# Batch 0's softmax denominators: summed two score tiles later, kept in the room of x's sums, the last group inside the projection

## The chip, the core and the metric

The kernel runs on one core of a Trainium2 chip. The metric is device microseconds of that core; lower is better. Everything is float32.

## What is computed

Two layers on x of shape (4, 1024, 32, 32): four batches, 1024 channels, 1024 tokens each. Only the first layer matters here.

```python
qkv = (x @ w_qkv.T + b_qkv).reshape(B, N, 3, nh, hd)      # 16 heads of 64
q, k = rmsnorm(rope(q)) * q_norm_w, rmsnorm(rope(k)) * k_norm_w
scores = einsum('bqhd,bkhd->bhqk', q, k) * hd ** -0.5
attn = softmax(scores, axis=-1)                           # exp / sum of exp
ctx = einsum('bhqk,bkhd->bqhd', attn, v)
out = rmsnorm(ctx @ w_proj.T, norm_out_w) + residual
```

The second layer (1x1, 3x3 and 1x1 convolutions with batch norms) follows and is not touched.

## The kernel before

Per batch the kernel projects q, k and v (two levels of a Strassen-like scheme, 49 products a matrix from batch 1 on), runs attention, and projects the result (y). Batch b's stages follow each other on PE.

**Attention** (`attention`, called once for each half c of the queries) loops over eight pairs of heads, hp = 0 to 7, so batch 0 has sixteen steps of this kind. In a step PE makes eight score tiles `sc` (keys 128t on, both heads, 512 queries; L781), ACT turns each into exponentials `p` (L788), and VectorE (DVE) adds the eight tiles into a sum `den` (L799 once, L801 six times). Then PE multiplies the exponentials by v into `cx` (L810), ACT copies it out, and GpSimd (POOL) adds the two halves by a DMA (L820).

The exponentials are not divided. Instead the sums are inverted beside the work, and the context is scaled later. In batch 0 this goes by **groups of two steps**, eight groups. After the second step of a group a function is put into the list `late`. The next step takes it out at its second score tile (t == 1): PE sums `den` over the partitions into the PSUM tile `dn` (`sums_of_four`, eight records at L863), ACT copies it to `rec` (L910), and `to_few` sends it to memory (L898, `densf<-rec`) and reads it back spread over 128 partitions (L902, `few<-densf`). Both DMAs are issued by SyncE's queue (SP). At the end of that step DVE inverts `few` (L914). SP writes it back (L915) and reads it into two broadcast tiles `inv` (L932). At the end of the step after that, DVE and POOL scale the context (`mean_of_v`, L764 and L765).

The last group of a batch goes another way (`last_inverses`): `dn` directly behind the last `cx`, copy on ACT (L923), reciprocal on DVE (L924), and DMAs from POOL's queue (L925, L932). Its scaling stands in the projection, at `after(3, means)`.

**Beside the attention of batch 0** the kernel prepares weights for later stages. A part is four 256 KB pieces: SP loads them into a ring of eight buffers (L406, L383), DVE makes four sums (L409 to L412, L392 to L395), POOL writes the four results to memory (L414, L397). `load_parts`, at t == 3, keeps two parts loaded ahead. So a load waits until POOL's DMA has read the buffer's previous content.

**What sets the order.** PE, POOL, DVE and ACT run their instructions in the order in which the program states them. SP is not among these: the planner chooses the order of SP's DMAs when the program is built. That order is then fixed, and SP works through it one by one: a DMA that waits holds up those behind it.

**Rooms.** `den` is a tile of the pool `acc` (tag "tot", two buffers). x's sums T0, T1 and T2 (pool `tp`) are used by the projections of q, k and v, and are free during the attention. In batches 1 to 3 the first half's `den` tiles already stand in T0 and T2 (`fold`). PSUM has three tiles of two banks for `sc`, which `dn` also takes, and one for `cx`; in the projection there are four banks `o1` and four banks `o2`.

**The projection behind the attention** (`project2` for y) starts with two products p1 and p2 on old data. Product `S2` (k == 2) reads sums of the context (`to`, L281 to L284). Half of these need the last steps' scaled context. `after(n, step)` puts a step into a list of due times, and `product_done` runs those that are due after each product. SP loads the products' weights `w_y` through the same ring of eight buffers, and at the same time the next batch's x (L215), whose room holds the exponentials until the last sum and the last `cx` are done.

Of the kernel before, what the change touches and what calls it, by code (L numbers as in the profile page):

```python
# [11 lines left out]
F32 = mybir.dt.float32  # L12
# [6 lines left out]
P = 128  # L19
# [5 lines left out]
CH = 512  # L25
# [36 lines left out]
NH = NT // 2  # L62
# [23 lines left out]
def program(ctx, tc, x, wblk, w2, w3, vecs, cos, sin, out, bad):  # L86
# [71 lines left out]
    with tc.tile_pool(name=f"st{u}", bufs=2) as st, ExitStack() as s:  # L158

        tp = s.enter_context(tc.tile_pool(name=f"tp{u}", bufs=1))  # L160
# [42 lines left out]
        def bank(kind, name):  # L203
            pool, shape = psum[kind]
            return pool.tile(shape, F32, tag=kind, name=name)
# [48 lines left out]
        def after(n, step):  # L254
            later.append((pace["at"] + n, step))
# [508 lines left out]
            nc.vector.tensor_tensor(cx, cx, w, ALU.mult)  # L764
            engine.tensor_scalar(cx, cx, col("bv", hp), None, ALU.add)  # L765

        def attention(b, c, q_all, k_all, v, probs_, late, ready, extra, slow, steps_in_all, load_parts, fold, then):


            at = half[c]  # L770
            sums_, contexts = [], []
            for hp in range(NHP):
                n = f"{b}_{c}_{hp}"
                rows = shifts(q_all, k_all, n, hp, c) if bad is None else None
                probs = []
                for t in range(N // P):
                    p = probs_[:, t]
                    sc = bank("sc", f"sc_{n}_{t}")
                    for keys in (low, high):
                        for j, d in enumerate((low, high)):  # L780
                            nc.tensor.matmul(  # L781
                                sc[keys, j], k_all[d, hp, t * P + keys.start : t * P + keys.stop], q_all[d, hp, at],
                                start=True, stop=bad is not None,
                            )
                    if bad is None:
                        for j in range(2):
                            nc.tensor.matmul(sc[:, j], ones[0:1, :], rows[j], start=False, stop=True)
                    nc.scalar.activation(p, sc, AF.Exp)  # L788
                    if t == 1:
                        if late:  # L790
                            late.pop(0)()
                        if fold and hp % 2 == 0:
                            d_ = fold[hp // 4][:, hp % 4 // 2 * 2 : hp % 4 // 2 * 2 + 2, :]
                        else:
                            d_ = acc.tile([P, 2, CH], F32, tag="tot", name=f"den_{n}")
                    if t == 3:
                        load_parts()
                    if t == 1:
                        nc.vector.tensor_tensor(d_, probs[0], p, ALU.add)  # L799
                    elif t > 1:  # L800
                        nc.vector.tensor_tensor(d_, d_, p, ALU.add)  # L801
                    probs.append(p)
                if (c, hp) == (NCH - 1, NHP - 1):
                    then()
                o = bank("cx", f"cx_{n}")
                for t in range(N // P):
                    for j in range(2):
                        h0 = (2 * hp + j) * HD
                        for i, keys in enumerate((low, high)):
                            nc.tensor.matmul(  # L810
                                o[j * HD : (j + 1) * HD, i], v[keys, t, h0 : h0 + HD], probs[t][keys, j],
                                start=(t == 0), stop=(t == N // P - 1),
                            )

                cx = q_all[:, hp, at]
                nc.scalar.copy(cx, o[:, 0])  # L816
                if b == 0 and (c, hp) != (NCH - 1, NHP - 1):
                    other = temp(f"cx_{n}")
                    nc.scalar.copy(other, o[:, 1])
                    nc.gpsimd.dma_start(cx, other, accum_op=ALU.add)  # L820
                else:
                    contexts.append((cx, o[:, 1]))
                sums_.append(d_)
                if hp % 2 == 1:
                    for r in ready:
                        mean_of_v(q_all, *r)
                    ready.clear()
                if fold:
                    halve(hp, d_, fold[hp // 4][:, hp % 4 // 2 * 2 : hp % 4 // 2 * 2 + 2, :])
                    if hp % 4 == 3:  # L830
                        eights.append((hp + 2, lambda n=n, hp=hp: sum_of_eight(b, n, hp, fold[hp // 4], ready)))
                if half_done and half_done[0][0] <= c * NHP + hp:
                    half_done.pop(0)[1]()
                if slow:
                    slow.pop(0)()

                if waiting:
                    next_waiting()
                slots = NCH * NHP - 1
                if extra and steps_in_all == 0 and hp > 0:  # L840
                    extra.pop(0)()
                for _ in range(len(extra) - -(-steps_in_all * max(slots - 1 - c * NHP - hp, 0) // slots) if steps_in_all else 0):
                    extra.pop(0)()
                if contexts:
                    nc.vector.tensor_tensor(contexts[0][0], *contexts.pop(0), ALU.add)
                if eights and eights[0][0] <= c * NHP + hp:
                    eights.pop(0)[1]()
                if hp % 2 == 0 or fold:
                    continue
                if (c, hp) == (NCH - 1, NHP - 1):  # L850
                    last_inverses(b, c, hp, n, sums_of_four(n, sums_), ready)
                else:
                    late.append(lambda n=n, hp=hp, ds=sums_: inverses(b, c, hp, n, sums_of_four(n, ds), ready))
                sums_ = []

        def sums_of_four(n, sums_):
            if n == f"0_{NCH - 1}_{NHP - 1}":
                bank("sc", f"skip_{n}")
            dn = bank("sc", f"dn_{n}")[:, 0]
            for i, d_ in enumerate(sums_):  # L860
                for j in range(2):
                    q = slice((2 * i + j) * QH, (2 * i + j + 1) * QH)
                    nc.tensor.matmul(dn[q, :], ones[:, :QH], d_[:, j], start=True, stop=True)  # L863
            return dn
# [55 lines left out]
        def last_inverses(b, c, hp, n, dn, ready):  # L920
            k = 2 * ((b * NCH + c) * NHP + hp - 1)
            r = temp(f"rec_{n}")
            nc.scalar.copy(r, dn)  # L923
            nc.vector.reciprocal(r, r)  # L924
            nc.gpsimd.dma_start(dens[k : k + 4, :], r[::QH, :])  # L925
            spread(c, hp, n, ready, [dens[k + j : k + j + 3 : 2, :] for j in range(2)], nc.gpsimd)
# [263 lines left out]
        for b in range(B):  # L1190
            units = units_of(room)
            q_all = kv.tile([P, NT, N], F32, tag="q", name=f"q_{b}")
# [16 lines left out]
            k_all = kp.tile([P, NT, N], F32, tag="k", name=f"k_{b}")  # L1209
# [10 lines left out]
            v = room  # L1220
# [15 lines left out]
            def load_parts():  # L1236

                while todo and len(made) < 2:
                    made.append(todo.pop(0)(pieces, nc.sync))

            extra = [lambda: made.pop(0)()] * len(todo)
            load_parts()
            late, ready, steps_in_all = [], [], len(extra)
# [7 lines left out]
            slow = [lambda: None] * 3 + [lambda f=f: add_residual(f) for f in range(NT)] if b > 0 else []  # L1251
            probs_ = xp.tile([P, N // P, 2, CH], F32, tag="x", name=f"p_{b}")
            fold = [None, None]
            if b > 0:

                fold[0] = [tp.tile([P, NH, CH], F32, tag=t, name=f"den_{b}_{t}") for t in ("T0", "T2")]
            tc_, two = [], []

            def then(b=b, q_all=q_all, tc_=tc_, two=two):
                yt[b] = kp.tile([P, NT, N], F32, tag="k", name=f"y_{b}")  # L1260
                two += [2, *in_place(q_all, tc_, yt[b], False), False]
                for part in range(2):
                    inner_sums(two[1], two[2], 0, part)

            for c in range(NCH):
                if (b, c) == (B - 1, NCH - 1):
                    extra = filters()
                attention(
                    b, c, q_all, k_all, v, probs_, late, ready, extra, slow, steps_in_all, load_parts, fold[c], then
                )  # L1270
            psum_for("proj")
            room = v_room(f"to_{b}")
# [166 lines left out]
        for f in range(NPT):  # L1439
            for c in range(NCH):  # L1440
                then = (first_channels, other_channels)[f] if c == NCH - 1 else None
# [139 lines left out]
        for f in range(NT):  # L1581
# [8 lines left out]
            for i, k in order:  # L1590
                b, c = divmod(i, NCH)
# [14 lines left out]
            sc, sh = norms[f] = norm_of(stats, col("g3", f), col("be3", f), f"3_{f}")  # L1606
# [81 lines left out]
```

## Time and profile before

| what | us |
|---|---|
| three runs | 2668.44, 2664.51, 2668.72 (median 2668.44) |
| the profiled execution | 2665.42, of which its span 2663.6 |
| attention of batch 0, first score tile to last `cx` | 288.6 to 518.2 |
| y projection of batch 0 behind it | 521.7 to 609.1 |
| 285 to 525: busy PE / DVE / ACT / POOL | 238.6 / 220.8 / 141.7 / 90.1 |
| mean share of the DMA engines there | 0.79 |

A line of the timeline gives the start, the time until the end of the group's last instruction, the engine, the source line, the operation, what it writes and reads, the count, and in brackets the idle time ahead of it with what ended it. For SP the idle time is not given: it is read from the starts. A line of the waits gives who waited for whom, the total in us, how often, and the longest. A busy PE is not a PE at its peak: a matmul's end is modelled, so a pause under half a microsecond is not seen as idle time, but in the starts.

### The profile page before, as it was taken

How to read it: one execution, taken by the hardware profiler on the slowest of the kernel's cores; microseconds unless marked ns; L12 is line 12 of the kernel's file. 1: busy time of each engine (PE TensorE's matmuls, PEld its weight loads, DVE VectorE, ACT ScalarE, POOL GpSimd, SP SyncE). 2: the span in 40 equal slices, each digit the busy share in tenths (PEclk: the TensorE clock that was granted, in tenths of full speed). 3: DMA queues.
4: the chain of work that ended last, by engine and by line, in shares of the span. 5: the costliest groups of instructions: out<-in, count | busy, mean ns of one | idle time of the engine just before them, and what ended most of it. 6: DMA issues, size and time to landing. Idle time of an engine off the chain costs nothing.

```text
span 2663.6 us, 40534 instructions
## 1 busy us (share of the span) xinstructions
PE 2628.3 (99%) x15434; PEld 1626.0 (61%) x15434; DVE 2142.2 (80%) x2595; ACT 1120.1 (42%) x1568; POOL 473.4 (18%) x592
## 2 busy tenths in 40 slices
PE   9999999999999999999999999999999999999997
PEld 4448533488888333588886333888884335846843
DVE  5577899988787977788888767887988778877987
ACT  2222465523342655333343655233425654312266
POOL 2542244301001221100111222000111221020000
PEclk9999999999999999999999999999999999999999
DMA  7887788867677452457776541765774443583165
GB/s 271 292 259 214 209 253 240 271 184 242 174 184 215 82 105 48 152 153 221 190 187 162 97 83 28 210 200 180 194 212 90 84 105 132 155 278 100 64 235 208
DMA packets 252793, 463.65 MB, mean 174 GB/s; under 512 B 32176, under 2 KB 124896, under 8 KB 252592
## 3 DMA queue, kind: packets, MB, share of 16 engines
q1 hardware_dynamic: 204736, 304.58, 36.9%
q0 software_dynamic: 47856, 156.40, 23.5%
q8 instruction: 125, 2.05, 0.3%
q14 instruction: 76, 0.62, 0.1%
HBM read 329.53 MB, written 97.01 MB: 160 GB/s over the span
## 4 chain that ended last, share of the span: by engine, by line
PE 66%; DVE 1%; DMA 1%; ACT 0%; issue 0%; ACTq 0%
PE sc L781 13%; PE cx L810 12%; PE p_y L485 9%; PE p_v L480 8%; PE p_k L485 6%; PE p_q L485 6%; PE c L1592 4%; PE c2x L1453 2%; PE c L1015 2%; PE c2y L1453 2%; PE c L974 1%; PE c1s L1015 1%; DMA w_y<-wdf 1%; PE dn L863 0%; DVE V L1388 0%; PE c1a L1015 0%
## 5 line engine op out<-in xcount | busy, mean ns | idle before, releaser
L788 ACT ACTIVATE p<-sc 128x1024 f32<-128x1024 f32 x512 | 478.1, 1049 | 17.8 <-PE sc L781 17.2
L781 PE MATMUL sc<-q,k 64*64 64x512 f32 x4096 | 456.2, 591 | 0.0
L801 DVE TENSOR_TENSOR den<-den,p 128x1024 f32<-128x1024 f32 x312 | 385.6, 1236 | 37.9 <-ACT p L788 5.1
L810 PE MATMUL cx<-p,to 64*64 64x512 f32 x3072 | 338.2, 589 | 0.0
L781 PEld LDWEIGHTS sc<-q,k 64*64 64x64 f32 x4096 | 149.7, 132 | 293.6 <-ACT p L788 149.5
L810 PEld LDWEIGHTS cx<-p,to 64*64 64x64 f32 x3072 | 117.5, 133 | 212.1 <-issue 211.0
L485 PE MATMUL p_y<-q,w_y 128*128 128x256 f32 x928 | 209.8, 379 | 0.7 <-issue 0.7
L480 PE MATMUL p_v<-w_v,x 128*128 128x256 f32 x928 | 209.9, 379 | 0.3 <-DVE x L451 0.3
L485 PEld LDWEIGHTS p_y<-q,w_y 128*128 128x128 f32 x928 | 176.0, 190 | 27.9 <-issue 4.1
L480 PEld LDWEIGHTS p_v<-w_v,x 128*128 128x128 f32 x928 | 176.1, 190 | 25.4 <-DVE x L451 1.2
L816 ACT COPY q<-cx 128x512 f32<-128x512 f32 x64 | 37.5, 585 | 348.1 <-PE cx L810 348.1
L765 POOL TENSOR_SCALAR q<-q,vec 128x512 f32<-128x512 f32 x56 | 110.4, 1985 | 290.5 <-DVE q L764 290.4
L485 PE MATMUL p_q<-to,w_q 128*128 128x256 f32 x672 | 152.2, 379 | 0.0
L485 PE MATMUL p_k<-to,w_k 128*128 128x256 f32 x672 | 152.2, 379 | 0.0
L485 PEld LDWEIGHTS p_k<-to,w_k 128*128 128x128 f32 x672 | 127.4, 190 | 18.4 <-issue 1.2
L485 PEld LDWEIGHTS p_q<-to,w_q 128*128 128x128 f32 x672 | 127.4, 190 | 18.4 <-issue 1.2
L810 PE MATMUL cx<-p,rq 64*64 64x512 f32 x1024 | 112.7, 589 | 0.0
L1592 PE MATMUL c<-h,w 128*128 128x512 f32 x256 | 110.3, 592 | 0.5 <-ACT h L1495 0.5
L485 PE MATMUL p_y<-to,w_y 128*128 128x256 f32 x384 | 90.8, 381 | 9.4 <-issue 5.4
L799 DVE TENSOR_TENSOR den<-p 128x1024 f32<-128x1024 f32 x52 | 63.5, 1222 | 42.5 <-ACT p L788 42.5
L801 DVE TENSOR_TENSOR den_T<-den_T,p 128x1024 f32<-128x1024 f32 x72 | 88.2, 1225 | 7.9 <-DVE den_T L801 0.5
L480 PE MATMUL p_v<-w_v,t 128*128 128x256 f32 x384 | 90.2, 379 | 0.1
(497 smaller groups left out, 4304.8 us busy)
## 6 DMA issues: line engine op xcount, KB each, us to landing
w_v<-wd2f SPq DMA_DIRECT2D x112, 256.0 KB, 3.1
w_y<-wd2f SPq DMA_DIRECT2D x112, 256.0 KB, 2.6
w_q<-wd2f SPq DMA_DIRECT2D x84, 256.0 KB, 2.7
w_k<-wd2f SPq DMA_DIRECT2D x84, 256.0 KB, 2.8
wd2f<-w_pre POOLq DMA_DIRECT2D x68, 256.0 KB, 4.5
x<-in_x_dram SPq DMA_DIRECT2D x64, 256.0 KB, 4.9
q<-qs POOLq DMA_DIRECT2D x64, 256.0 KB, 5.4
k<-ks POOLq DMA_DIRECT2D x64, 256.0 KB, 4.6
```

What stands on the lines that cost most here:

```text
L480: nc.tensor.matmul(o[:, q].rearrange("p (g f) -> p g f", g=2), r[:, i, q * P : (q + 1) * P], wt[:, :, i, :], skip_group_check=True, **at,)
L485: nc.tensor.matmul(o[:, q], wt[:, q, i, :], r[:, i, :], skip_group_check=True, **at)
L765: engine.tensor_scalar(cx, cx, col("bv", hp), None, ALU.add)
L781: nc.tensor.matmul(sc[keys, j], k_all[d, hp, t * P + keys.start : t * P + keys.stop], q_all[d, hp, at], start=True, stop=bad is not None,)
L788: nc.scalar.activation(p, sc, AF.Exp)
L799: nc.vector.tensor_tensor(d_, probs[0], p, ALU.add)
L801: nc.vector.tensor_tensor(d_, d_, p, ALU.add)
L810: nc.tensor.matmul(o[j * HD : (j + 1) * HD, i], v[keys, t, h0 : h0 + HD], probs[t][keys, j], start=(t == 0), stop=(t == N // P - 1),)
L816: nc.scalar.copy(cx, o[:, 0])
L1015: nc.tensor.matmul(o, wt[:, i, :], rows(i), start=first and i == 0, stop=last and i == NH - 1, skip_group_check=True,)
L1453: nc.tensor.matmul(o[:, r * TR * TC : (r + 1) * TR * TC], uw[2 * h + r, j][:, i * PL + f * P : i * PL + (f + 1) * P], vt[b, i][:, 2 * h + ...
L1592: nc.tensor.matmul(os[i], w3t[k][f // NH][:, f % NH, :], h2[b, k][:, half[c]], start=(k == 0), stop=(k == NPT - 1),)
```

## The change

It touches batch 0's attention alone. (1) The function in `late` is taken out at t == 3 in place of t == 1, ahead of `load_parts`. (2) The sums `den` of batch 0 stand in T0 and T2, two steps in each, in place of the two buffers of `acc`; four steps pass until a place is used again. (3) The last group's `dn`, copy, reciprocal and DMAs are put in the list of due times (`after(0.5, ...)`), so that they come behind the projection's first product; `dn` takes a bank of `o2`.

```diff
-        def attention(..., fold, then):
+        def attention(..., fold, then, own):
...
                     nc.scalar.activation(p, sc, AF.Exp)
+                    if t == (3 if b == 0 else 1) and late:
+                        late.pop(0)()
                     if t == 1:
-                        if late:
-                            late.pop(0)()
-                        if fold and hp % 2 == 0:
+                        if b == 0:
+                            d_ = own[hp % 4 // 2][:, hp % 2 * 2 : hp % 2 * 2 + 2, :]
+                        elif fold and hp % 2 == 0:
                             d_ = fold[hp // 4][:, hp % 4 // 2 * 2 : hp % 4 // 2 * 2 + 2, :]
...
                 if (c, hp) == (NCH - 1, NHP - 1):
-                    last_inverses(b, c, hp, n, sums_of_four(n, sums_), ready)
+
+                    def last(ds=sums_):
+                        last_inverses(b, c, hp, n, sums_of_four(n, ds), ready)
+
+                    if b == 0:
+                        after(0.5, last)
+                    else:
+                        last()
...
         def sums_of_four(n, sums_):
             if n == f"0_{NCH - 1}_{NHP - 1}":
-                bank("sc", f"skip_{n}")
-            dn = bank("sc", f"dn_{n}")[:, 0]
+                dn = bank("o2", f"dn_{n}")
+            else:
+                dn = bank("sc", f"dn_{n}")[:, 0]
...
+            own = None
+            if b == 0:
+                own = [tp.tile([P, NH, CH], F32, tag=t, name=f"den_{b}_{t}") for t in ("T0", "T2")]
```

More of the change, by code (lines that the diff above doesn't have):

```diff
@@ L765, in mean_of_v, with attention @@
             engine.tensor_scalar(cx, cx, col("bv", hp), None, ALU.add)
-        def attention(b, c, q_all, k_all, v, probs_, late, ready, extra, slow, steps_in_all, load_parts, fold, then):
+        def attention(b, c, q_all, k_all, v, probs_, late, ready, extra, slow, steps_in_all, load_parts, fold, then, own):
             at = half[c]
@@ L1268, in program @@
                 attention(
-                    b, c, q_all, k_all, v, probs_, late, ready, extra, slow, steps_in_all, load_parts, fold[c], then
+                    b, c, q_all, k_all, v, probs_, late, ready, extra, slow, steps_in_all, load_parts, fold[c], then, own
                 )
```

## The prediction

> **What bounds the kernel now.** I read first the page's busy times, then batch 0's attention alone (busy times from 285 to 525 us).
>
> ```profile
> PE 2628.3 (99%) x15434; PEld 1626.0 (61%) x15434; DVE 2142.2 (80%) x2595; ACT 1120.1 (42%) x1568; POOL 473.4 (18%) x592
> ```
> ```profile
> 285.00:525.00 240.00, 238.61 (x2144) 83.39 (x2144) 220.76 (x234) 141.65 (x170) 90.11 (x121) 1.00 0.79 239
> ```
>
> PE is the bound of the whole, but in this stage DVE is at 92%: with the small gaps between its instructions it is nearly full. In PE's starts a step without `dn` takes 13.75 us (6.88 of scores, 6.87 of `cx`) with no hole. So PE loses only at `dn`:
>
> ```profile
> 375.41 1.83 PE L863 MATMUL dn<-den,ones 128*32 128x512 f32 x8
> 377.16 5.38 PE L781 MATMUL sc<-q,k 64*64 64x512 f32 x48
> ```
> ```profile
> 518.23 1.05 PE L863 MATMUL dn<-den,ones 128*32 128x512 f32 x4
> 519.95 1.05 PE L863 MATMUL dn<-den,ones 128*32 128x512 f32 x4 [0.66 <-DVE den L801]
> 521.73 3.69 PE L485 MATMUL p_y<-q,w_y 128*128 128x256 f32 x16 [0.73 <-issue]
> ```
>
> From one start to the next, `dn` takes 1.00 us where `den` is ready (so at 318.06 and in batch 1, 1092.46 to 1093.46). Above it takes 1.75, and 3.50 in the last group. Over groups 1 to 7 the starts give 0.07 + 0.76 + 0.60 = 1.4 us of waiting, in the last group 2.5 us.
>
> Then I read the way of the sums to memory and back, for group 3: SP, DVE and POOL from 376 us on.
>
> ```profile
> 377.90 0.54 SPq L898 DMA_DIRECT2D densf<-rec  x1
> 385.59 1.55 SPq L383 DMA_DIRECT2D w_pre<-wdf  x3
> 387.23 0.42 SPq L902 DMA_DIRECT2D few<-densf  x1
> 387.74 0.38 SPq L383 DMA_DIRECT2D w_pre<-wdf  x1
> 390.89 0.33 SPq L915 DMA_DIRECT2D densf<-few  x1
> ```
> ```profile
> 379.71 1.06 DVE L395 TENSOR_TENSOR w_pre<-w_pre,w_pre 128x512 f32<-128x512 f32 x1
> 380.69 1.21 DVE L799 TENSOR_TENSOR den<-p 128x1024 f32<-128x1024 f32 x1
> 382.01 7.87 DVE L801 TENSOR_TENSOR den<-den,p 128x1024 f32<-128x1024 f32 x6
> 390.61 0.25 DVE L914 RECIPROCAL few<-few 128x16 f32<-128x16 f32 x1 [0.73 <-DMA few<-densf]
> ```
> ```profile
> 381.05 2.21 POOL L397 DMA_DIRECT2D wd2f<-w_pre  x4
> ```
> ```profile
> SPq L383 <- DMA wd2f<-w_pre: 56.5, 38, 7.1
> ```
>
> SP stands still from 378.4 to 385.6: its next load waits until POOL's write, issued behind DVE's sums that end at 380.8, has left the buffer. `densf` slipped out before that. DVE reaches its reciprocal at 389.9 and waits 0.7 us for `few`. The waits show the same for this load line in total (56.5 us). DVE's waits for `few` are 3.9 us in the stage: 2.0, 0.7 and 1.2 in groups 1, 3 and 4.
>
> **Part 1, `dn` at the fourth tile.** It issues the same eight matmuls, one copy and two SP DMAs a group. On PE the place is 1.7 us later (two tiles of 0.86), so the waits of 1.4 us go if DVE keeps its pace. The copy stands between exponentials 4 and 5; ACT is busy 8.8 us of a step of 14 to 15, so I cost it at nothing; without that cover it is 0.5 us a group (an idle time of 0.3 to 0.5 us behind `dn` is there today), 3.5 at most.
>
> What counts is SP. The copy now ends about two microseconds later, and in the built order of the changed kernel `densf` no longer stands ahead of the waiting loads. Group 1: behind three more `w_blk` loads. Group 2: unchanged. Groups 3, 6 and 7: behind all four `w_pre` loads, `few` directly after it. Groups 4 and 5: behind five loads, and `few` behind three more. Queued behind it on DVE, whose order is unchanged, is everything: reciprocal, weight sums, the next `den`, and PE's next `dn` for that. POOL's writes wait for the sums, and the next loads for these writes, so nothing is caught up: the time of each group counts from DVE's sums.
>
> Price: the last load ahead (its issue today; in group 3 at 387.3 without `few` in front of it), 0.5 us of SP for it, the trip of `densf`, the trip of `few`. The trip of `densf` is issue to issue where nothing else holds `few`: 1.8 (951.09 to 952.93), 2.2 at most in group 1, 4.7 in group 2 (348.54 to 353.22). The trip of `few` is 2.4 to 4.0 by the view of line L902 (its landings), and 6.1 in group 4 (415.31 to 421.39, when DVE starts). Ends: 1.8 + 2.4 and 4.7 + 6.1. I take 2.5 (near group 1: loads are just ahead of it) and 2.4 (the shortest, as nothing is issued behind the loads while DVE waits).
>
> | group | last load ahead | `few` lands | DVE there | wait then | wait now | added |
> |---|---|---|---|---|---|---|
> | 1 | 327.7 | 333.1 | 329.9 | 3.2 | 2.0 | 1.2 |
> | 3 | 387.3 | 392.7 | 389.9 | 2.8 | 0.7 | 2.1 |
> | 4 | `few` behind 419.8 | 422.7 | 420.2 | 2.5 | 1.2 | 1.3 |
> | 5 | `few` behind 448.9 | 451.8 | 450.5 | 1.3 | 0 | 1.3 |
> | 6 | 473.0 | 478.4 | 476.3 | 2.1 | 0 | 2.1 |
> | 7 | 502.0 | 507.4 | 505.1 | 2.3 | 0 | 2.3 |
>
> Sum 10.3 us. With the short trips (a few tenths less a group) it is 7, with the long ones 43 (7 to 8 in most groups). If `few` were never late, today's 3.9 us would go: -4.
>
> DVE late by 10 us makes PE late by about 8 to 10, as the room at t == 3 (`den` of the pair ends 0.4 to 3 us ahead of PE's new place) is used up once.
>
> The Trainium skill ("TensorE: Matmul & The Clock Gate", Part 1) says that an idle window of about 3.4 us halves PE's clock, for at least another such window; that speaks against any change that makes PE stop for longer. In this case a stop of 2.0 us (ahead of 1114.69) leaves the granted clock at 1.00; no trace here shows a longer one in these stages. By the rule a group with a stop over 3.4 us would pay up to 1.7 us more as an estimate, so nothing at the stops above and some 10 us in the worst of the rivals.
>
> **Part 2, the room.** The sums cost DVE the same (1225 ns each for `den_T`, L801, in the page). T0 and T2 were last read before the attention begins, and x's next sums come only at 558. A place is used again after four steps, so no wait is added: nothing. Bounds: 0.
>
> **Part 3, the last group in the projection.** `dn` still needs the last `den`, whose end (519.9) is DVE's. PE can do p1 before it: p2 starts at about 521.0 in place of 523.5, 2.4 us sooner. But that is not what ends the projection:
>
> ```profile
> 541.45 0.69 DVE L764 TENSOR_TENSOR q<-q,inv 128x512 f32<-128x512 f32 x1 [6.09 <-DMA inv<-densf]
> 545.55 1.23 DVE L282 TENSOR_TENSOR to<-q,to 128x1024 f32<-128x1024 f32 x1
> ```
> ```profile
> 546.88 1.97 PE L485 MATMUL p_y<-to,w_y 128*128 128x256 f32 x8 [1.32 <-issue]
> ```
>
> PE stands ahead of 546.88 until DVE's sum at 545.55 is done, that waits for the scaling, and that for `inv`, which landed just before 541.45. The reciprocal in front of it (L924, at 524.21) stands behind other work of DVE, not behind `dn`. So an earlier PE waits longer at the same place: 0 gained. Batch 1, which loses nothing at `dn`, shows these stops too (2.0 and 1.5 us). Bounds: -2.4 if `inv` came so much sooner, +2 if the loads that PE now releases sooner hold it up (in batch 1, `inv` takes 15.5 us from L925 on, here 13.6). I take +0.5.
>
> The skill ("TensorEngine Tiling (Array Packing)", Key Properties) says that a change of the tiling mode drains TensorE. Part 3 makes three such changes out of two, as `dn` (128x32) stands between two 128x128 products. The trace agrees: `dn`'s weight load waits 0.8 us for the score tile ahead, against 0.28 between two score tiles. So 0.5 us more on PE, covered by the same stop; the page gives no other price.
>
> **The sum.** The profiled execution took 2665.42 us, its span 2663.6; 2665.4 + 10.3 + 0.5 = 2676.2. The median of the runs shown is 3.0 higher, the mean of all four 2666.8. I take a point between: **2678**.
>
> **Rivals.**
> *In time after all (not slower).* Place: the reciprocal of `few` at L914. If both trips together take less than about 2.6 us in group 3 (389.9 less 387.3) and 2.8 in groups 6 and 7, DVE never waits, PE stops no more at `dn`, and `inv` ends the projection as now. That gives 2663 to 2669. For it: DMAs are quiet while DVE waits. Against it: no trip pair below 4.2 us is seen. Trips near 4 give gains and losses under 5.3 us, too: 2667 to 2673. Together 0.27, of which 0.05 below 2663.
> *Long trips.* Place: the same. If loads and POOL's writes slow both trips as in groups 2 and 4, up to 43 us, 2690 to 2712. For it: the DMA engines are busy 0.79. Against it: the 4.7 and the 6.1 fell beside writes of POOL that would be over. 0.10.
> *It does not do what it says.* The order gives PE room at `dn` that DVE takes away again; that is part of my forecast, not a case of its own.
> *Forecast*, 2673 to 2690: 0.63.
>
> A measurement here tells about 0.2% (5.3 us) from no change. Slower by more: 0.63 + 0.10 = 0.73. Within it: 0.22. Faster: 0.05. The range 2667 to 2689 leaves out about 0.10 above and 0.08 below.
>
> **What would show it.** Right: DVE's idle time ahead of L914 (then at another line) of 1 to 3 us in six of seven groups, SP's `densf` behind the loads, the last `den` ending near 530, PE waiting for `den` at `dn` again, and the stop ahead of the `S2` product longer. Wrong: `few` landed before DVE's sums are done, or the last `den` ending at 520 with a projection that ends sooner.

## The result, and the profile after

| kernel | median, us | runs | ratio to the kernel before |
|---|---|---|---|
| before | 2666.40 | 2662.65 to 2668.72 | |
| after | 2677.39 | 2675.18 to 2680.83 | 1.0045, 95% interval 1.0032 to 1.0058 |

The change makes the kernel slower by 0.45%. The profiled execution has a span of 2675.6 us against 2663.6, so 12.0 us more. Lines of the file move: `densf<-rec` is L908 now, `few<-densf` L912, the reciprocal L924, `densf<-few` L925; `dn` is L873, the first addition to `den_T` L801 and the others L803. The last group's reciprocal is L934, its DMAs are L935 and L942, and the last addition of the context is L847 (L845 before).

**Where the time came from.** I call *the stage* the time from batch 0's first score tile to the first product of q in batch 1. It takes 320.52 us before (288.60 to 609.12) and 335.22 after (288.27 to 623.49): 14.7 more. The last `den` ends at 534.46 in place of 519.89, so all of it is there when the attention ends. Behind the stage 3 us come back in batch 1's y projection, 88.65 us before and 85.64 after, which the change does not touch; in the runs below it takes 85.4 to 88.8.

Busy times of the attention again (the same window and columns as before the change; behind DVE's stand ACT's and POOL's, the granted clock, the DMA share and GB/s), and DVE's and SP's largest waits (who waited for whom, total, times, longest):

```profile
285.00:525.00 240.00, 233.31 (x2080) 78.85 (x2082) 206.43 (x219) 140.34 (x167) 88.05 (x117) 0.99 0.72 217
```
```profile
DVE few L924 <- DMA few<-densf: 19.8, 6, 5.9
```
```profile
SPq L383 <- DMA wd2f<-w_pre: 88.9, 56, 10.3
```

No engine does more work: in the same window DVE has 14.3 us less to do, PE 5.3, and the DMA engines went from 0.79 to 0.72. The work has moved out of the window because DVE stands still: 19.8 us for `few`, where it was 3.9. SP's waits for POOL's writes (line 383) have grown too, from 56.5 to 88.9: the writes wait for DVE's sums, and the sums for `few`.

Group 4 shows the whole chain, on SP, DVE and PE in that order:

```profile
417.80 0.94 SPq L908 DMA_DIRECT2D densf<-rec  x1
418.87 2.44 SPq L383 DMA_DIRECT2D w_pre<-wdf  x3
424.03 0.33 SPq L912 DMA_DIRECT2D few<-densf  x1
428.47 0.33 SPq L925 DMA_DIRECT2D densf<-few  x1
```
```profile
414.38 7.87 DVE L803 TENSOR_TENSOR den_T<-den_T,p 128x1024 f32<-128x1024 f32 x6
428.19 0.25 DVE L924 RECIPROCAL few<-few 128x16 f32<-128x16 f32 x1 [5.94 <-DMA few<-densf]
```
```profile
434.50 1.05 PE L873 MATMUL dn<-den_T,ones 128*32 128x512 f32 x4
440.33 1.92 PE L873 MATMUL dn<-den_T,ones 128*32 128x512 f32 x4 [4.79 <-DVE den_T L803]
442.19 5.39 PE L781 MATMUL sc<-q,k 64*64 64x512 f32 x28
```

`densf` goes out at 417.80, behind the loads of its step, and three more loads follow it. `few` is issued 6.2 us later and is there for DVE after 4.2 more. DVE has been ready since 422.2. Twelve microseconds later PE stands at the next `dn`, that of group 5, for 4.8 us, since the second `den_T` of its group is late by then. Look at the matmuls behind the stop, too: four of `dn` take 1.92 us where four took 1.05.

Then the end of the attention and the first products of the projection, on PE, and on DVE what they wait for:

```profile
533.12 1.05 PE L873 MATMUL dn<-den_T,ones 128*32 128x512 f32 x4
534.51 1.05 PE L873 MATMUL dn<-den_T,ones 128*32 128x512 f32 x4 [0.34 <-DVE den_T L803]
538.96 3.54 PE L485 MATMUL p_y<-q,w_y 128*128 128x256 f32 x8 [3.40 <-issue]
...
561.33 1.89 PE L485 MATMUL p_y<-to,w_y 128*128 128x256 f32 x8
```
```profile
538.18 0.68 DVE L847 TENSOR_TENSOR q<-q,cx 128x512 f32<-128x512 f32 x1
...
553.07 0.69 DVE L764 TENSOR_TENSOR q<-q,inv 128x512 f32<-128x512 f32 x1 [3.14 <-DMA inv<-densf]
...
557.18 1.22 DVE L282 TENSOR_TENSOR to<-q,to 128x1024 f32<-128x1024 f32 x1
```

The stop ahead of the second product of `to` (546.88 before) is gone: that product follows at 561.33 without idle time, well behind L282. In its place stands a new stop of 3.4 us ahead of p2. The page puts it down to nothing ("issue"). In the built program `dn` has taken the first bank of `o2`, p2 gets the next one, and that room held half of the last `cx`, which DVE's L847 reads until 538.8. p2 starts 0.1 us later, and its eight matmuls take 3.54 us in place of some 1.9.

### The profile page after: what moved, and what is told of

Same layout as the page of the kernel before. It is cut to its first block, busy times and chain, and to the rows that moved or that the text cites. A ratio compares the mean times of both kernels' runs of the same rounds, so it can differ in the third digit from the quotient of the medians.

```text
span 2675.6 us, 40529 instructions
## 1 busy us (share of the span) xinstructions
PE 2634.7 (98%) x15434; PEld 1627.5 (61%) x15434; DVE 2141.6 (80%) x2595; ACT 1121.3 (42%) x1568; POOL 475.2 (18%) x592
## 5 line engine op out<-in xcount | busy, mean ns | idle before, releaser
L803 DVE TENSOR_TENSOR den<-den,p 128x1024 f32<-128x1024 f32 x216 | 267.9, 1240 | 27.6 <-ACT p L788 5.1
L803 DVE TENSOR_TENSOR den_T<-den_T,p 128x1024 f32<-128x1024 f32 x168 | 205.8, 1225 | 17.5
L727 POOL DMA_DIRECT2D k<-ks x64 | 57.7, 1088 | 184.2 <-ACT p L788 71.1
```

Of the source, the lines that this page charges most:

```text
L727: nc.gpsimd.dma_start(dst[i::2, f, :], other[1 - i :: 2, :], accum_op=ALU.add)
```

## The experiments

Theory: `densf` and `few` stand too far back in SP's order, DVE's reciprocal waits, and all else follows. Rival 1: `dn` at the fourth tile costs by itself (ACT's copy, a score tile's room). Rival 2: the room T0/T2. Rival 3: part 3 costs, by the new stop at p2.

All of it in one table. "`dn`" is what the `dn` of groups 1 to 7 take over 7 x 1.0 us, "`inv`" the way from the issue of the last group's `densf` on POOL to DVE's use of `inv`.

| kernel | median, us | ratio, 95% interval | stage | DVE's wait for `few` | `dn` | `inv` |
|---|---|---|---|---|---|---|
| before | 2666.40 | | 320.5 | 3.9 | 1.4 | 13.6 |
| after | 2677.39 | 1.0045 (1.0032 to 1.0058) | 335.2 | 19.8 | 11.1 | 10.7 |
| e1_sp | 2663.96 | 0.9995 (0.9985 to 1.0005) | 320.2 | 0 | 0 | 9.6 |
| e3_no3 | 2681.03 | 1.0056 (1.0042 to 1.0069) | 335.0 | 19.2 | 7.2 | 11.4 |
| e5_densf_behind | 2682.02 | 1.0065 (1.0051 to 1.0079) | 339.9 | 25.3 | 15.1 | 10.0 |
| e7_before_sp | 2665.70 | 1.0008 (0.9999 to 1.0017) | 318.8 | 0 | 0.9 | 12.0 |
| e2_o1 | 2683.17 | 1.0064 (1.0050 to 1.0077) | 336.3 | 19.3 | 9.5 | 14.7 |
| e6_sp_o1 | 2668.04 | 1.0009 (1.0000 to 1.0018) | 321.3 | 0 | 0 | 13.5 |
| e8_sp_no3 | 2665.06 | 1.0000 (0.9991 to 1.0009) | 318.6 | 0 | 0 | 12.9 |
| e9_sp_part3_o1 | 2669.90 | 1.0016 (1.0007 to 1.0026) | 324.4 | 0 | 1.5 | 14.4 |
| e10_x_later | 2660.08 | 0.9985 (0.9976 to 0.9994) | 315.6 | 0 | 0 | 7.6 |
| e11_before_x_later | 2664.30 | 0.9994 (0.9985 to 1.0003) | 317.9 | 0 | 0.5 | 8.3 |

Each ratio is to the kernel before, run beside it.

The last four columns come from one profiled execution of each kernel. How far such figures vary is seen where the attention is the same: from the first score tile to the end of the last `den` it takes 244.4 to 246.2 us after the change and in e2_o1 and e3_no3, 230.3 to 231.5 in e7, e9 and e11, and 229.8 to 230.1 in e1, e6, e8 and e10. (It is 231.3 before and 250.4 in e5.) What follows the stage takes 2052 to 2061 us in these executions, so differences of a few microseconds between medians cannot be read from the stage alone.

### e1_sp: the whole change, with densf and few ahead of the loads

```diff
+            in_order = ExitStack()
+            if b == 0:
+                in_order.enter_context(tc.manual_schedule(engines={mybir.EngineType.SP}))
             for c in range(NCH):
...
                 attention(...)
+            in_order.close()
```

> The changed kernel, all three parts, with one difference: during batch 0's attention SP issues its DMAs in the order in which the program states them, so that densf and few stand ahead of the waiting weight loads again. The orders of PE, ACT, DVE and POOL are those of the changed kernel. Theory (few is late because densf stands behind the loads; DVE's waits for few are 19.8 us in the changed kernel, 3.9 in the kernel before): the waits fall to 0 to 4 us, the last den ends at 515 to 521 in place of 534.5, and the time is 2660 to 2668. Rival 1 (dn at the fourth tile itself is what costs, by ACT's copy between two exponentials or by the score tile's room in PSUM): the last den still ends at 528 or later, 2673 to 2680. Rival 3 (the last group inside the projection costs, with PE's new wait ahead of p2 and the half clock behind it, 3.4 + 1.7 us): the attention is quick, but 5 us stay, 2669 to 2672.

Measured: 2663.96 us, the last `den` at 518.17, no wait for `few` at all, and every one of the seven `dn` takes 1.00 us. The first product of the projection starts 228.2 us after the first score tile; before it was 233.1, after 243.0. Rival 1 falls, and rival 2 with it, as the new room of the sums is in this kernel. What stays is the stop ahead of p2, as rival 3 has it, though the total is the theory's:

```profile
516.53 1.99 PE L485 MATMUL p_y<-q,w_y 128*128 128x256 f32 x8
518.46 1.06 PE L873 MATMUL dn<-den_T,ones 128*32 128x512 f32 x8
522.67 3.75 PE L485 MATMUL p_y<-q,w_y 128*128 128x256 f32 x8 [3.15 <-issue]
```

PE is at p1 5 us sooner than before (3.5 of them because `dn` now stands behind p1) and loses nearly all of it here: p2 starts 234.3 us after the first score tile, before the change 234.9. So the stage takes what it took before (320.2).

### e5_densf_behind: the kernel before, with only densf and few behind the loads

```diff
                     if t == 3:
                         load_parts()
+                        if sends:
+                            sends.pop(0)()
...
-            few, rows = to_few(n, k, 4, r[::QH, :])
+            def send():
+                few, rows = to_few(n, k, 4, r[::QH, :])
...
+            if b == 0:
+                sends.append(send)
+            else:
+                send()
```

(With `in_order` as in e1_sp; the inversion is queued inside `send`.)

> The kernel before with its dn at the second tile, its den tiles and its last group untouched; only the two DMAs densf and few of each group are issued behind the weight loads of the step, and SP works in the order of the program. Theory (this place in SP's queue is the cost): DVE waits 8 to 20 us for few in the stage where the kernel before waits 3.9, the last den ends at 525 to 536 in place of 519.9, and the time is 2673 to 2685. Rivals 1 and 2 (the place of dn on PE and ACT, or the room of the sums): none of their edits is in it, so 2664 to 2669.

Measured: 2682.02 us, the waits for `few` 25.3 us, the last `den` at 537.52. The time is in the range of the theory; the waits and the last `den` are beyond it (8 to 20 us, 525 to 536). None of the change's edits is in this kernel, and it loses more than the change. On SP in group 3:

```profile
373.69 15.91 SPq L383 DMA_DIRECT2D w_pre<-wdf  x9
389.69 0.54 SPq L900 DMA_DIRECT2D densf<-rec  x1
```

`densf` is issued at 389.69 behind nine loads, the last of which wait for POOL's writes. So this place in SP's order makes the loss by itself.

### e7_before_sp: the control

```diff
+                in_order.enter_context(tc.manual_schedule(engines={mybir.EngineType.SP}))
```

(The `in_order` lines of e1_sp, in the kernel before.)

> Control: the kernel before, with SP in the order of the program during batch 0's attention and nothing else. Theory: densf and few stand ahead of the loads as they do now, so the time is that of the kernel before, 2662 to 2669, with waits for few of 0 to 5 us. If SP's order by itself, apart from densf and few, moves the time, it shows here: under 2660 or over 2671, and then the other runs with this order are to be read against this one.

Measured: 2665.70 us, as before. SP in group 3, for comparison with e5 above and with the lines of the kernel before in the prediction:

```profile
375.87 0.54 SPq L898 DMA_DIRECT2D densf<-rec  x1
379.04 0.33 SPq L902 DMA_DIRECT2D few<-densf  x1
383.60 2.15 SPq L383 DMA_DIRECT2D w_pre<-wdf  x4
```

Both small DMAs are out before the loads begin to wait, and DVE never waits for `few`. `dn` is at 0.9 us over its floor in place of 1.4, with `dn` still at the second tile. Whether `few` had a part in those waits stays open: e9 and e11, with this same attention and no wait for `few` either, show 1.5 and 0.5.

### e3_no3: parts 1 and 2 alone

```diff
-                    if b == 0:
-                        after(0.5, last)
-                    else:
-                        last()
+                    last()
...
-                dn = bank("o2", f"dn_{n}")
-            else:
-                dn = bank("sc", f"dn_{n}")[:, 0]
+                bank("sc", f"skip_{n}")
+            dn = bank("sc", f"dn_{n}")[:, 0]
```

> The changed kernel without its part 3: the last group's dn stands directly behind the last cx again, ahead of the projection; parts 1 and 2 stay. Theory (the loss is made in the attention, by few): the last den ends at 531 to 537 as in the changed kernel, DVE's waits for few are 16 to 22 us, and the time is 2673 to 2681. Rival 3 (part 3 costs, by PE's wait ahead of p2 and the half clock): 2672 or less, at least 5 us below the changed kernel.

Measured: 2681.03 us, the last `den` at 531.36, 19.2 us of waits for `few`. The loss is made by parts 1 and 2 under the new order on SP. The stage takes 335.0 us, with part 3 335.2: part 3 neither costs nor gains here. The medians differ by 3.6 us, but the intervals of the two ratios overlap.

### e2_o1: another bank for the last dn

```diff
-                dn = bank("o2", f"dn_{n}")
+                dn = bank("o1", f"dn_{n}")
```

> The changed kernel with one word changed: the last group's dn takes a bank of o1 in place of o2, so that p2 gets the bank that it had in the kernel before and need not wait for DVE's last addition of the context (L847). The orders of all engines stay. Theory (PE's stop ahead of p2, 3.4 to 4.0 us, is that bank, and the half clock behind it, 1.7 us, comes from the stop): p2 starts at 535 to 536 in place of 538.96 at full clock; of these 5 us about 2 are lost again ahead of the second product of to (which needs DVE's sum L282, done at 558.4), so the time is 2 to 4 us under the changed kernel, 2672 to 2676. Rival (p2 waits for something else: the tiling mode, its weights, the last den): p2 stays at 538 to 539.5, and the time at 2675 to 2680.

Measured: 2683.17 us; both the theory's number and the rival's miss. p2 starts at 538.55, inside the rival's range, but not for the rival's reason: it does follow `dn` directly (537.55, then 538.55), as the bank would have it. p1 itself stood 4.26 us for its weights and ran at half clock. Then PE stopped for 2.1 and 2.2 us ahead of the two products of `to`. The profile puts the first stop down to a load of `w_y`; the second ends with DVE's sum L282 (563.23), which came late as `inv` took 14.7 us in place of 10.7. The stage is 1.1 us longer than after the change. The medians differ by 5.8 us, with overlapping intervals; the rest lies behind this stage and I have no cause for it.

### e6_sp_o1: both mendings

The edits of e1_sp and e2_o1 together.

> The changed kernel with both mendings: SP in the order of the program in batch 0's attention (as in e1_sp) and dn of the last group in a bank of o1. Theory: no wait for few, PE without a stop up to dn, p2 at 519.4 to 520.0 in place of 522.7 in e1_sp and at full clock. In e1_sp the second product of to stood 5.4 us behind the end of DVE's sum L282, so up to 4.8 us can come through: 2658 to 2662 us, 2 to 5 under e1_sp and under the kernel before. Rival (what PE gains by p2 is lost ahead of the products of to, to their weights w_y or to inv): 2662 to 2666, as e1_sp, with a stop of 1 us or more ahead of a product of to.

Measured: 2668.04 us. That is 6 us above the theory's range; the rival's mechanism is there, at more than its price. p2 starts at 519.95 with no stop and at full clock, 2.7 us sooner than in e1_sp. PE then meets this, with DVE's line under it:

```profile
545.85 3.75 PE L485 MATMUL p_y<-to,w_y 128*128 128x256 f32 x8 [4.91 <-issue]
```
```profile
540.42 0.69 DVE L764 TENSOR_TENSOR q<-q,inv 128x512 f32<-128x512 f32 x1 [6.03 <-DMA inv<-densf]
```

`inv` took 13.5 us in place of 9.6, so the sum that the product needs (L282) began 4.7 us later than in e1_sp. Whatever PE had gained is lost at the place that the prediction named as the end of the projection, and the half clock behind the stop (3.75 us for eight matmuls) takes some more. I had taken `inv` as fixed. It is not: it depends on what PE does.

### e8_sp_no3 and e9_sp_part3_o1: one part alone, few in time

e8 is e1_sp with the edit of e3_no3; e9 is e7_before_sp with part 3 and a bank of `o1`.

> The changed kernel with SP in the order of the program and without part 3 (the last group's dn directly behind the last cx, as in the kernel before); parts 1 and 2 stay. Theory: part 1 costs nothing when few is in time, and gains little, as the waits at dn are already gone when only SP's order is that of the program (dn takes 1.0 to 1.6 us in e7_before_sp): 2662 to 2667 us, within 2 us of e7_before_sp. Rival 1 (dn at the fourth tile costs by itself): 2668 or more. Rival 3 (part 3 is the part that is worth something): 2 to 5 us over e6_sp_o1.

> The kernel before (dn at the second tile, den in its own buffers) with SP in the order of the program and with part 3 alone, dn of the last group in a bank of o1. Theory: part 1 is worth 1 us at most once few is in time, so this is e6_sp_o1 without it: 2658 to 2664 us, at most 2 us over e6_sp_o1. Rival (part 1 and the room are what carries e6_sp_o1, by PE's waits at dn): 2664 to 2667, as e7_before_sp.

Measured: e8 2665.06 us, as e7_before_sp, so parts 1 and 2 cost nothing once `few` is in time; at the start of the projection they bring 1.0 us (232.0 against 232.9 from the first score tile on), which is also about the distance of e7, e9 and e11 from e1, e6, e8 and e10 in the attentions compared under the table. Rival 3 of e8 misses: it is 3 us under e6_sp_o1, not over it, with ratios that overlap. e9 took 2669.90 us, outside what I expected of it and of the rival: PE is at p1 3.3 us sooner than in e7_before_sp, stops for 6.1 us ahead of the second product of `to`, and `inv` takes 14.4 us. In the stage part 3 without its stop ahead of p2 costs 5.6 us (324.4 against 318.8); the medians are 4.2 us apart, the intervals of the two ratios overlap a little.

### e10_x_later and e11_before_x_later: what makes inv long

The DMA share during `inv`'s way was 0.78 in e1_sp (9.6 us), 0.82 after the change (10.7), 1.06 in e6_sp_o1 (13.5), 1.04 in e9 (14.4) and 1.00 before (13.6). SP's lines show what runs there: loads of the next batch's x (L215) and of `w_y`, issued as PE frees their rooms. Where PE stops ahead of p2 they come later: in e1_sp SP issues no load of x from 521 to 526.8. So these two kernels load x five products later:

```diff
-                    after(3 + 1.5 * j, load)
+                    after((8 if b == 0 else 3) + 1.5 * j, load)
...
-                    after(3 + 1.5 * (2 * i + 3) + 2, queue)
+                    after((8 if b == 0 else 3) + 1.5 * (2 * i + 3) + 2, queue)
...
             ty = qk_proj(b, WP, q_all, tc_, None, yt[b], "y", None, two)
+            in_order.close()
```

(e10 in e6_sp_o1, e11 in e7_before_sp; `in_order` is closed here in place of behind the attention. So SP's order in the projection and the times of x's sums on DVE change along with the loads; no run separates the three.)

> e6_sp_o1 with the next batch's x loaded later: the due times of its loads and of its sums are five products later, and SP keeps the order of the program through batch 0's y projection too, so that no load of x stands ahead of inv's way through memory. Theory (in e6_sp_o1 and e2_o1 that way took 13.5 and 14.7 us because loads of x ran beside it; it took 9.5 and 10.6 where PE's stop ahead of p2 held these loads back): from the issue of densf to DVE's use of inv 8 to 10.5 us, the 5.3 us gap ahead of the second product of to falls to 0 to 1.5 us, and the time is 2659 to 2664. Rival (the way is long whatever runs beside it, or the w_y loads alone make it so): 12 us or more, the gap stays at 4 to 6 us and the time at 2665 to 2670. A third way: the late x costs at the start of q of batch 1, 2670 or more.

> The kernel before with SP in the order of the program (as e7_before_sp) and the same later loads of x, with none of the change's three parts. Theory: inv's way takes 8 to 10.5 us, so the gap of about 1.0 to 1.7 us ahead of the second product of to goes, but PE's 1 us wait at the last dn stays: 2661 to 2666 us, 1 to 4 over e10_x_later, which has 3 us less ahead of p2. Rival (part 1 and part 3 are worth nothing even then): within 1 us of e10_x_later.

Measured: e10 2660.08 us, e11 2664.30. Ten microseconds of `inv`'s way, first e6_sp_o1, then e10, with DMA share and GB/s at the end of the line:

```profile
526.00:536.00 10.00, 10.00 (x48) 8.83 (x47) 8.25 (x10) 1.98 (x5) 1.84 (x3) 1.00 1.06 359
```
```profile
526.00:536.00 10.00, 10.00 (x48) 8.81 (x47) 9.72 (x14) 2.35 (x4) 1.84 (x3) 1.00 0.74 205
```

The first loads of x that SP issues from 515 us on, in the same two kernels:

```profile
518.98 1.29 SPq L215 DMA_DIRECT2D x<-in_x_dram  x3
```
```profile
540.79 0.91 SPq L215 DMA_DIRECT2D x<-in_x_dram  x2
```

And e10's second product of `to`, with the scaling on DVE:

```profile
540.14 1.89 PE L485 MATMUL p_y<-to,w_y 128*128 128x256 f32 x8
```
```profile
533.59 0.69 DVE L764 TENSOR_TENSOR q<-q,inv 128x512 f32<-128x512 f32 x1
```

PE does the same in both, with the same number of matmuls in the window. Without the loads of x `inv` is there after at most 7.6 us (DVE does not wait for it), and no product of `to` up to 545 waits. With that, the stage is 315.6 us, 2.4 less than in e11, which has the later x alone (their medians are 4.2 us apart, the intervals of the ratios overlap). That parts 1 and 3 are then worth something is likely, not shown. The third way of the expectation is there in small: both kernels with the later x have a stop of 1.05 us early in q of batch 1 (ahead of 608.45 in e10, of 611.28 in e11) that e6 and e7 do not have. And e10's profiled execution is its slowest, 2664.52 us; its span is only 0.9 us under that of the kernel before, though its stage is 5 us shorter. By its median e10 is the fastest kernel of this study, 0.15% under the kernel before (interval 0.06% to 0.24%) and, by the two ratios, some 0.6% under the changed one (0.9985 / 1.0045 = 0.994).

## Why the prediction was right, point by point

- **What bounds, and the mechanism** (DVE's reciprocal of `few` behind loads on SP): right. e1_sp takes this one thing away and the loss is gone; e5_densf_behind adds it alone and makes a loss; in e7_before_sp SP's order without that leaves the time as it was.
- **The table of added waits**: 10.3 us forecast, 15.9 measured (19.8 less 3.9). The mis-sized term is the two trips in groups 4 and 5. By group, forecast and measured: 1.2 and 2.0; 2.1 and 0.9; 1.3 and 4.8; 1.3 and 4.1; 2.1 and 2.9; 2.3 and 1.3. In groups 4 and 5 I had let `few` follow the last load and priced its own trip alone, at 2.4 us, "as nothing is issued behind the loads while DVE waits"; the trip of `densf` does not appear there. But `few` was issued only 6.2 and 5.2 us after `densf`, more than the 2.5 that I took elsewhere and the 4.7 that I had set aside for a rival, and its own trip took 4.2 and 3.3. The three loads that were issued between the two do not explain it: in e5_densf_behind `few` directly follows `densf`, and groups 4 and 5 still take 4.9 and 4.8. What they go with is the DMA share during the trip: 1.04 and 1.07 after the change, 0.99 and 1.07 in e5, against 0.55 to 0.77 in groups 1, 3, 6 and 7 after the change (2.4 to 3.2 us). So the DMA engines were not quiet there, as the rival "in time after all" supposed. No run tests this link by itself. Two bounds are added up wrongly: by the table's own rows the short trips give 7.5 in place of 7, the long ones 41 in place of 43. The forecast does not hang on them.
- **"PE late by about 8 to 10"**: the last `den` ends 14.6 us later, for 15.9 us of waits. It was to end near 530 and ends at 534.5. PE does wait for `den` at `dn` again, and DVE ahead of the reciprocal in six of seven groups, for 1.3 to 5.9 us each in place of the 1 to 3 that I gave.
- **Clock gate, "nothing at the stops above"**: wrong, as the stops were longer than my table had them. The stop behind group 4's late `few`, in the `dn` of group 5, was 5.4 us from start to start, and behind it the granted clock is 0.53 from 440.4 to 447. What that costs in the attention no run separates; behind p2 it costs 1.7 us (3.54 for eight matmuls in place of some 1.9).
- **ACT's copy and the room, nothing**: right (e1_sp, e8_sp_no3).
- **Part 3, +0.5, with a longer stop ahead of the second product of `to`**: the sum is right (from the last `den` to q of batch 1 89.2 us before, 89.0 after), the step is not. I did not look at which bank p2 would get. The stop moved to p2, and with it `inv`'s way took 10.7 us, where I had forecast it longer; that the sum came out is luck. The 0.5 us for the tiling mode was near: in e6_sp_o1, where nothing waits, matmul starts are 0.31 us apart going into `dn` and 0.52 coming out of it, against 0.22 inside a product, so 0.4 more together. That x's loads can hold `inv` up is the bound of +2 that I gave; in e6_sp_o1 and e9 the way is long again, 13.5 and 14.4 us, and e10 points to these loads.
- **The sum**: 2678 forecast, 2677.4 measured. It is closer than its parts, by luck: the stage is 4 us longer than I had it, and 3 us came back in batch 1's y projection, where the kernels are the same.
- **The rival "in time after all"**, 2663 to 2669: it is what happens in e1_sp (2664.0), and its condition, `few` there before DVE's sums are done, was the right one.

## What to carry to other kernels

When work is moved on one engine, read where its DMAs come to stand in every queue that they pass, before its cost on the engine itself: two 8 KB transfers behind loads that wait cost 11 us, and stating them ahead of these loads takes the loss away. A place gained on the busiest engine was worth nothing here until the next due event moved too; that was `inv`, and it moved only when the next batch's loads were held back. Ask of every PSUM bank that is taken in a new place which bank the next product gets, and who still reads it.

## What the runs showed of the hardware

Stops of PE are given from one matmul's start to the next, the clock as granted, from 100 us on to the last matmul in all twelve profiles. No stop of up to 2.35 us lowered the clock by itself, and every one of 2.71 to 6.1 us did, to 0.50. Between these both happened: 2.39 us in e3_no3 and 2.44 in e6_sp_o1 lowered it, 2.41 in e8, 2.47 in e5, 2.49 after the change, 2.57 in e1 and 2.66 in e2 did not. Two stops of nearly the same length, in the y projection of batch 1 in e6_sp_o1 and of batch 2 in e8_sp_no3, show it in the time of the eight matmuls behind them:

```profile
1116.28 3.54 PE L485 MATMUL p_y<-to,w_y 128*128 128x256 f32 x8 [2.06 <-DMA w_y<-wdf]
```
```profile
1681.29 2.00 PE L485 MATMUL p_y<-to,w_y 128*128 128x256 f32 x8 [2.03 <-DMA w_y<-wdf]
```

So the length of a stop alone does not decide between 2.4 and 2.7 us. Each stretch at 0.50 lasted 3.4, 6.8 or 10.2 us: 3.4 behind the 2.44 in e6_sp_o1, 6.8 behind a stop of 3.74 in e1_sp, 10.2 in e3_no3 around stops of 5.79 and 1.79. The Trainium skill ("TensorE: Matmul & The Clock Gate", Part 1) gives about 3.4 us of idle time for the drop. The stops of 2.39 to 3.12 us that lowered the clock are below that, so here the measurement decides.

The way of an 8 KB block to memory and back as a broadcast (`inv`) took 7.6 to 8.3 us at a DMA share of 0.76 to 0.77, 9.6 to 10.7 at 0.78 to 0.82, 10.0 to 14.7 at 0.90 and 12.0 to 14.4 at 0.96 to 1.06. The share does not order them alone: the 10.0 and the 14.7 both had 0.90. I had not expected that a stop of PE might pay for itself by keeping such a transfer's way free: e1_sp, with the stop ahead of p2, has a stage of 320.2 us, no longer than that of e6_sp_o1 without it (321.3).
